# Products of a zero matrix in the open sums of attention 1 and of the convolution of a two-layer graph network

## The chip, the cores and the metric

The kernel runs on one core of one Trainium2 chip. The metric is the time of one launch in microseconds, taken on the device; lower is better. The median of 10 runs of the kernel before is 4104.61 us (lowest 4102.45, highest 4113.44).

## The reference, cut to what matters

A graph has 6250 nodes with 128 features and 200000 edges that are sorted by their destination. Two layers follow each other, both with a residual sum. The first is a graph attention network of two attention layers, the second a convolution over edges:

```
h = relu(layernorm(x))
# attention 1: 4 heads of 16;  attention 2: 1 head of 128
msg = feat[src] * softmax_by_dst(leaky_relu(el[src] + er[dst]))
x = x + segment_sum(msg, dst)                    # (after both attention layers)
h = relu(layernorm(x))
# convolution
w   = einsum(W_tp, gelu(gelu(edge_attr_8 @ W_mlp1) @ W_mlp2))     # weights by edge
mid = concat(m0, m1, m2, m3)       # w * feat[src] * edge_attr_4, 256 numbers by edge
agg = zeros(N, 256).at[dst].add(mid)
x = x + cos * self(h) + sin * (agg @ Wf)
```

The sums over edges by destination (`segment_sum`, `.at[dst].add`) are what the change touches: they are made on TensorE, as products of a 0/1 matrix (edge by node) with the messages, summed in PSUM.

## The kernel before, in words

The edges are cut into tiles of 128, and 8 tiles are a group (`SB = 8`). The rows of the source nodes are fetched by gathers of one tile each, issued by GpSimd (POOL): `gather`, L349 to L353, the issue itself at L351.

**Attention 1** (to about 1590 us of the profile) runs over 117 groups, cut into 8 micro-steps each (`for now in range(NGR * MS + MS)`, L1197). All engines follow the order in which the program is written, recorded under `manual_schedule`; no engine but TensorE's weight loads reorders anything. Three kinds of work are interleaved by micro-step:

- The messages of the group by gathers. `message` (L386) on VectorE (DVE) makes them, ScalarE (ACT) rounds them to a high half (L1226), DVE makes the low half (L1230), `expanded` (L383) gives each edge its node's numbers, `hot` (L356) the 0/1 matrix, and `scatter` (L1154, the product at L1159) adds the group's 8 tiles into the PSUM tile `kept1["acc"]`, 128x136. A chunk of 16 tiles (two groups) is one open sum; when it closes, `evict` copies it by ACT (L1165) and adds it by DVE (L1167). The open sum has one buffer.
- Tables of counts of edges between blocks of nodes: `compare` on DVE (L851), four products a bank on TensorE (L877), eviction by ACT into `ca` (L859), and a DMA to memory (L863). The result of the products has two PSUM buffers, `ca` two in SBUF.
- Dense attention for the other blocks, from the counts: `ramps`, with ACT (L1095), DVE (`clip`, L1019) and TensorE (`add`, L1010 and L1013), and at the end of a pass `close` (L1025, L1027) and `end` (L1040, L1044, L1046). `finish1` (L885 onwards, products L901 and L908) ends four blocks.

In a micro-step the order is: the gathers (m = 0 only), the eviction of a closed sum, the counts' products, the ramps, then `expanded` (m = 3), `hot` (m = 5), `scatter` of one or two tiles of the group before (m = 2 to 7), and the chains of small steps.

**Attention 2** (about 1590 to 2133 us) is dense: TensorE products with bf16 weights at L1414.

**The convolution** (2133 us to the end) runs over 196 groups. For a group, POOL issues 8 gathers (L351), ACT scales the rows (L1494), TensorE makes the hidden layers (`hidden`, L1475) three groups ahead and the weights by edge (`weigh`, L1487) two groups ahead, DVE and ACT make the messages (L1507 to L1541), and `scatter` (L1552) adds the 8 tiles into `state["acc"]`, 128x512 in PSUM. After 24 tiles (`CT`) the sum closes: `close` copies it by ACT (L1582), and `finish3` (L1560 to L1569) transforms it, adds the residual and stores. `sink` tells for each tile whether it starts and whether it closes the sum. Here too the order is that of the program. Per group TensorE has: the first hidden layer of group g + 3, a step of `finish3` if one is due, the second hidden layer, `weigh` of g + 2, and the 8 products of `scatter`. There are six buffers for gathered rows.

```
            first = layers(g + 3)
            next(first, None)
            if not last:
                rows = fetch(g + 1)
            next(first, None)
            pw = big() if hids or todo else None
            if todo:
                todo.popleft().send(pw)
```

Of the kernel before, what the change touches and what calls it, by code (L numbers as in the profile page):

```python
# [32 lines left out]
BF16 = mybir.dt.bfloat16  # L33
# [10 lines left out]
P = 128  # L44
SB = 8
# [3 lines left out]
WSTEP = 16  # L49
HS = 7  # L50
CT, LT = 24, 40
DENSE1 = 20
LAG_D, AFTER, AFTER_D = 14, 12, 5
GP, GK, GSB = 125, 16, 4
# [9 lines left out]
def gnn_kernel(ctx: ExitStack, tc: tile.TileContext, x, src, dst, attr4, attr8,  # L64
# [3 lines left out]
    nc = tc.nc  # L68
# [5 lines left out]
    HD = W1.shape[1]  # L74
    H1, DH = al1.shape
# [17 lines left out]
    NT = src_t.shape[1]  # L93
    NG = NB - DENSE1
    HALF = P // 2
# [16 lines left out]
    keep = tc.keep_in_program_order  # L112

    def big():
        return ps_big.tile([P, 8, P], F32, tag="big", name="big")
# [10 lines left out]
    def whole():  # L126
        return ps_acc.tile([P, 512], F32, tag="acc", name="whole")
# [53 lines left out]
    def load_weights(*pairs):  # L181
        tiles = []
        for name, w in pairs:
            tiles.append(const.tile(list(w.shape), F32, name=name))
            nc.sync.dma_start(tiles[-1], w)
        return tiles
# [488 lines left out]
    keep = lambda ins: ins  # L675
# [40 lines left out]
    def fetch_rows(g):  # L716
        G[g] = gath.tile([P, SB, R1], F32, tag="G", name="G")
        gather(G[g], table1, srcw[:, g * SB:(g + 1) * SB], SB)
# [20 lines left out]
    aw = one.enter_context(tc.tile_pool(name="aw", bufs=2, reuse_waits="tile"))  # L739
# [15 lines left out]
    rhs1 = [dram.tile([P, NB, HW], BF16, name=f"rhs1{q}") for q in range(H1 // 2)]  # L755
    deg1 = pool.tile([P, DENSE1], F32, name="deg1")

# [199 lines left out]
    HH = H1 // 2 * C1  # L957
    assert DENSE1 % 4 == 0
    passes = [(b0, q) for b0 in range(NG, NB, 4) for q in range(H1 // 2)]
# [165 lines left out]
    kept1 = {}  # L1125
# [7 lines left out]
    def chunk_of(g):  # L1133
        return (g * SB + HT // 2) // HT

    def first_of(c):
        return max(0, HT * c - HT // 2)

    def last_of(c):
        return HT * c + HT // 2  # L1140
# [13 lines left out]
    def scatter(g, tiles):  # L1154
        c = chunk_of(g)
        if tiles[0] == 0 and g * SB == first_of(c):
            kept1["acc"] = whole()[:, :2 * (HD + H1)]
        for t in tiles:
            nc.tensor.matmul(kept1["acc"], ohs[g][:, t, :], mss[g][:, t].rearrange("e s f -> e (s f)"),  # L1159
                             start=g * SB + t == first_of(c), stop=g * SB + t + 1 == last_of(c))  # L1160

    def evict(c):
        acc = kept1["acc"]
        ring = fin.tile([P, HD + H1], F32, name="ring", bufs=2)
        nc.scalar.copy(ring, acc[:, :HD + H1])  # L1165
        yield
        nc.vector.tensor_add(ring, ring, acc[:, HD + H1:])  # L1167
        if c:
            b = (c - 1) // 2
            part = slice(0, HALF) if c % 2 else slice(HALF, P)  # L1170
            if c % 2 and b % 4 == 0:
                kept1["sums"] = fin.tile([P, 4, HD + H1], F32, name="sums1", bufs=2)
            nc.vector.tensor_add(kept1["sums"][part, b % 4, :], kept1["ring"][part], ring[part])
            if c % 2 == 0 and (b % 4 == 3 or b == NG - 1):
                chains[0].append(finish1(b // 4 * 4, b % 4 + 1, kept1["sums"][:, :b % 4 + 1, :]))
        kept1["ring"] = ring

    NGR, MS = NT1 // SB, 8
    LEAD = 4
    for c in chunks[:2]:  # L1180
# [16 lines left out]
    for now in range(NGR * MS + MS):  # L1197
        g, m = divmod(now, MS)
        if m == 0 and g + LEAD < NGR:
            fetch_rows(g + LEAD)  # L1200
        if m == 0 and g == 10:
            lin, wm1_sb, wm2_sb, wtp_sb, wf_sb = load_weights(*late_weights)
        done = g >= 2 and (g - 1) * SB == last_of(chunk_of(g - 2))
        if m == 0 and done:
            leaving = evict(chunk_of(g - 2))
            next(leaving)
        due = min(n_banks, n_banks * (now + 1) // ((NGR - AFTER) * MS))
        for _ in range(due - banks):
            next(counting)
        banks = due  # L1210
        if m == 0 and done:
            deque(leaving, 0)
        due = min(n_ramps, max(0, n_ramps * (now + 1 - LAG_D * MS)) // ((NGR - LAG_D - AFTER_D) * MS))
        if due and ramping is None:
            ramping = ramps()
        for _ in range(due - ticks):
            next(ramping)
        ticks = due
        if due == n_ramps:
            next(ramping, None)  # L1220
        if g < NGR:
            if m == 1:
                msg = message(G.pop(g), pes.pop(g))
            if m == 2:
                mss[g] = aw.tile([P, SB, 2, HD + H1], F32R, name="halves")
                nc.scalar.copy(mss[g][:, :, 0, :], msg)  # L1226
            if m == 3 and g + 1 < NGR:
                expanded(g + 1)
            if m == 4:
                nc.vector.tensor_tensor(mss[g][:, :, 1, :], msg, mss[g][:, :, 0, :], op=OP.subtract)  # L1230
            if m == 5 and g + 1 < NGR:
                hot(g + 1)
        if g and m >= 2:
            scatter(g - 1, ((0, 1), (2, 3), (4,), (5,), (6,), (7,))[m - 2])
        for chain in chains:
            advance(chain)
        if evens is None and banks == n_banks:
            assert len(written) == len(steps)
            building.close()
            evens = ahead2.enter_context(tc.tile_pool(name="evens", bufs=1, side="right", reuse_waits="tile"))  # L1240
            pair0 = pair_counts([evens], 0, [nc.sync] * 2), pair_logits([evens], 0)
# [5 lines left out]
    keep = plain  # L1247
    nc.vector.tensor_scalar(wtp_sb[:, 0:3, :], wtp_sb[:, 0:3, :], 1.0 / math.sqrt(HID), None, op0=OP.mult)
    nc.vector.tensor_scalar(wtp_sb[:, 3, :], wtp_sb[:, 3, :], 1.0 / math.sqrt(3.0 * HID), None, op0=OP.mult)
    written_order.close()  # L1250
    nc.vector.tensor_tensor(over1[:, NG:], over1[:, NG:], miscounted(pool, deg1, n_edges[:, NG:], DENSE1), op=OP.max)
    again, some = flags(pool, over1, wide1.to_broadcast([1, NB]))
# [10 lines left out]
    tiles = ctx.enter_context(tc.tile_pool(name="tiles", bufs=1))  # L1263
# [47 lines left out]
    with tc.tile_pool(name="att2", bufs=1) as pool, tc.tile_pool(name="dense", bufs=2) as dense, \  # L1311
# [68 lines left out]
        for b0 in range(0, NB, 2):  # L1380
            n = min(2, NB - b0)
# [10 lines left out]
            acc = big().rearrange("p (k a) c -> p k (a c)", k=2)  # L1392
            if b0 == 8:
                load_tiles(pool)
            for h0 in range(0, NB, HS):
# [7 lines left out]
                c = ct[:, :n, :, h0:h0 + HS, :].rearrange("p k a h d -> p h (k a) d")  # L1403
# [7 lines left out]
                for j, made in ((0, up), (1, down)):  # L1411
                    for h in range(HS):
                        for k in range(n):
                            nc.tensor.matmul(acc[:, k, j * C2:(j + 1) * C2], made[:, h, k * P:(k + 1) * P],  # L1414
                                             rhs2[:, h0 + h, j, :],
                                             start=h0 + h + j == 0, stop=h0 + h + j == NB)
                next(behind, None)
            parts = dense.tile([P, 2, 2, R2], F32, name="parts")
            acc = acc[:, :n, :2 * C2].rearrange("p k (j c) -> p k j c", j=2)
# [30 lines left out]
    cw = ctx.enter_context(tc.tile_pool(name="cw", bufs=2))  # L1450
# [93 lines left out]
    def one_hot3(dl, n, oh):  # L1544
        keep(nc.vector.tensor_tensor(oh[:, :n, :], slot[:, None, :].to_broadcast([P, n, P]),
                          dl[:, :, None].to_broadcast([P, n, P]), op=OP.is_equal))
        return oh

    def scatter(ms, oh, cs, sink):
        for c in cs:  # L1550
            acc, start, stop = sink(c)
            keep(nc.tensor.matmul(acc, oh[:, c, :], ms[:, c].rearrange("e s h i u -> e (s h i u)"), start=start, stop=stop))  # L1552
# [19 lines left out]
    with tc.tile_pool(name="conv", bufs=1) as pool, tc.tile_pool(name="gath3", bufs=6) as gath:  # L1572
# [4 lines left out]
        state, todo = {}, deque()  # L1577
# [12 lines left out]
        def sink(t):  # L1590
            c, k = divmod(t, CT)
            end = min(CT, NT - c * CT) - 1
            if k == 0:
                state["acc"] = whole()
            if k == min(6, end) and c:

                same = cw.tile([P, P], F32, name="same")
                keep(nc.vector.tensor_scalar(same, slot, shift[:, c - 1:c], None, op0=OP.is_equal))
                for a in state["sums"]:
                    keep(nc.tensor.matmul(state["acc"][:, :2 * D], same, a, start=False, stop=False))  # L1600
            return state["acc"], k == 0, k == end

        groups = [(t, min(SB, NT - t)) for t in range(0, NT, SB)]

# [47 lines left out]
        for g, (t, n) in enumerate(groups):  # L1652
            G, g0 = rows
            i = t % LT
            last = g + 1 == len(groups)
            ms, after = messages(G, g0, n, a1s[:, i:i + n, :], pws.popleft(), None if last else lambda: hots(g + 1),
                                 lambda: hids.extend(list(second)[-1:]))
            if i + SB == LT and t + SB < NT:
                a1s = keep_a1(t + SB)
            first = layers(g + 3)  # L1660
            next(first, None)
            if not last:
                rows = fetch(g + 1)
            next(first, None)
            pw = big() if hids or todo else None
            if todo:
                todo.popleft().send(pw)
                next(first, None)
            if t and t % CT == 0:
                close(t // CT - 1)  # L1670
            if hids:
                pws.append(weigh(groups[g + 2][1], hids.popleft(), pw))
            next(first, None)
            scatter(ms, oh, range(n), lambda c: sink(t + c))
            second = first
            oh = after
# [118 lines left out]
```

## Time and profile before

| | |
|---|---|
| median of 10 runs | 4104.61 us |
| the profiled execution | 4109.72 us |
| its span, first to last instruction | 4108.0 us |
| mean granted TensorE clock over the span | 0.812 |
| TensorE busy with products | 2990.8 us (73%) |
| DVE, ACT, POOL busy | 3589.0 (87%), 2791.4 (68%), 2638.6 us (64%) |

The profile is one execution. PE is TensorE's products, PEld its weight loads, SP the queue that issues DMAs. A row of the groups view names the line, the engine, what is written and read, and the number of instructions; then its busy time and the mean time of one, then the idle time of the engine just before them and what ended it. PEclk is the share of TensorE's full clock that was granted. In the records behind it the clock is either 1.0 or 0.5, in stretches that are whole multiples of 3.413 us; such a piece is called a window in what follows.

### The profile page before, as it was taken

To read this page: it belongs to the slowest core of one execution; us is meant where nothing else is said; L and a number is where in the kernel's file an instruction comes from. 1 tells how busy PE (TensorE), PEld (TensorE's weight loads), DVE (VectorE), ACT (ScalarE), POOL (GpSimd) and SP (SyncE) were. 2 spreads that over 40 slices of the span, in tenths; PEclk is the share of its full clock that TensorE was granted. 3 is DMA by queue.
4 is the path that set the end of the run, shared out by engine and by line. 5 is a ranking of instruction groups with operands and counts; after the bars stand their busy time and mean duration, and the time that the engine had idled before them with its cause. 6 is when DMAs were issued, how large, how long until landed. Compare 5 with 4: busy or idle time off the path is not lost. (4 is left out here: it accounts for less than half of the span.)

```text
span 4108.0 us, 61327 instructions
## 1 busy us (share of the span) xinstructions
PE 2990.8 (73%) x19231; PEld 2109.9 (51%) x19232; DVE 3589.0 (87%) x6074; ACT 2791.4 (68%) x6317; POOL 2638.6 (64%) x2568
## 2 busy tenths in 40 slices
PE   4456667676666766999977777777777777777777
PEld 3344445444444446888854444444444444444444
DVE  6888988998888877999969998989998998988997
ACT  3458878887778775999966655555555555555655
POOL 5777877777777770000017777777777777777775
PEclk8557877787777777999988888888888888888888
DMA  4556766776666665444422222222222222222221
GB/s 120 143 168 186 189 168 174 193 186 179 173 166 182 182 180 190 161 166 168 173 79 61 63 62 63 62 62 63 62 63 62 64 62 62 63 62 63 62 62 48
DMA packets 391299, 482.40 MB, mean 117 GB/s; under 512 B 237609, under 2 KB 273300, under 8 KB 390950
## 3 DMA queue, kind: packets, MB, share of 16 engines
q1 hardware_dynamic: 307780, 332.00, 26.7%
q0 software_dynamic: 82400, 144.35, 15.2%
q8 instruction: 159, 2.61, 0.3%
q10 hardware_dynamic: 770, 1.88, 0.2%
q14 instruction: 190, 1.56, 0.1%
HBM read 374.52 MB, written 103.42 MB: 116 GB/s over the span
## 5 line engine op out<-in xcount | busy, mean ns | idle before, releaser
L351 POOL DMA_INDIRECT G<-table,srcc x1563 | 1474.8, 944 | 1018.1 <-DVE kept L1458 542.0
L351 POOL DMA_INDIRECT G<-table,srcw x936 | 1098.7, 1174 | 294.8 <-issue 274.6
L1095 ACT ACTIVATE up<-erb,sel 128x512 bf16<-128x512 f32 x980 | 689.5, 733 | 0.0
L877 PE MATMUL small<-key,lo 128*128 128x98 bf16 x3136 | 339.1, 243 | 254.7 <-ACT ca L859 232.5
L1552 PE MATMUL whole<-halves,ohr 128*128 128x512 f32 x1563 | 501.4, 459 | 0.7 <-ACT acc L1582 0.7
L1494 ACT ACTIVATE g<-G,a 128x128 f32<-128x128 f32 x1563 | 484.4, 393 | 11.1 <-DMA G<-table,srcc 9.1
L859 ACT CAST ca<-small 128x392 bf16<-128x392 f32 x784 | 380.6, 489 | 158.5 <-DMA counts<-ca 100.0
L1010 PE MATMUL up<-up,rc 128*102 128x512 bf16 x980 | 444.9, 475 | 46.1 <-DVE up L1019 20.7
L1401 ACT ACTIVATE ramp<-erb,sel 128x256 bf16<-128x256 f32 (+1 forms) x1138 | 458.2, 493 | 14.4 <-DVE up L1409 9.3
L1487 PEld LDWEIGHTS big<-wtp_sb,hid 64*128 64x128 f32 x3126 | 266.7, 252 | 362.7 <-issue 341.6
L877 PEld LDWEIGHTS <-lo 128*128 128x128 bf16 x3136 | 245.9, 118 | 363.7 <-issue 329.9
L1487 PE MATMUL big<-wtp_sb,hid 64*128 64x128 f32 x3126 | 309.2, 353 | 140.6 <-DVE halves L1541 140.1
L1552 PEld LDWEIGHTS whole<-halves,ohr 128*128 128x128 f32 x1563 | 314.1, 208 | 127.4 <-issue 53.2
L1159 PE MATMUL whole<-halves,ohr 128*128 128x136 f32 x936 | 371.9, 450 | 9.7 <-DVE ring L1167 9.7
L1478 ACT ACTIVATE hid<-layer 128x512 f32<-128x512 f32 x392 | 230.6, 588 | 191.1 <-PE layer L1475 191.1
L1475 PE MATMUL layer<-a8t,wm_sb 16*128 16x512 f32 x392 | 231.6, 672 | 161.8 <-ACT hid L1478 151.8
L1475 PE MATMUL layer<-hid,wm_sb 128*128 128x512 f32 x392 | 337.7, 959 | 14.6 <-ACT hid L1478 12.9
L1532 ACT CAST halves<-mess 128x512 fp32r<-128x512 f32 x195 | 114.3, 586 | 329.8 <-DVE mess L1519 329.8
L1524 DVE TENSOR_TENSOR halves<-mess,halves 128x512 fp32r<-128x512 f32 x391 | 267.8, 685 | 60.2 <-ACT halves L1527 46.9
L1019 DVE TENSOR_TENSOR up<-up,ctc 128x3584 bf16<-128x3584 bf16 x140 | 282.2, 2016 | 28.7 <-ACT up L1095 17.0
L1159 PEld LDWEIGHTS whole<-halves,ohr 128*128 128x128 f32 x936 | 225.5, 259 | 55.2 <-issue 24.9
L1537 ACT CAST halves<-big 128x1024 fp32r<-128x1024 f32 x196 | 197.8, 1009 | 80.5 <-DVE big L1535 80.5
(306 smaller groups left out, 6338.3 us busy)
## 6 DMA issues: line engine op xcount, KB each, us to landing
counts<-ca SPq DMA_DIRECT2D x196, 392.0 KB
ct<-counts SPq DMA_DIRECT2D x196, 392.0 KB
ctc<-counts SPq DMA_DIRECT2D x1120, 56.0 KB
oht<-dlow SPq DMA_DIRECT2D x58, 512.0 KB
rc<-rhs SPq DMA_DIRECT2D x70, 358.8 KB
G<-table,srcc POOLq DMA_INDIRECT x1563
G<-table,srcw POOLq DMA_INDIRECT x936
a8t<-attr_rows SPq DMA_DIRECT2D x391, 16.0 KB
```

The costliest lines, as they stand in the source:

```text
L351: nc.gpsimd.indirect_dma_start(out=G[:, c, :], out_offset=None, in_=table, in_offset=bass.IndirectOffsetOnAxis(ap=idx[:, c:c + 1], axis=0))
L859: nc.scalar.copy(ca[:, :, k * W:(k + WBANK) * W].rearrange("p h (k d) -> p h k d", d=W), ps[:, :WBANK * NKEY].rearrange("p (k h d) -> p h ...
L877: nc.tensor.matmul(ps[:, n * NKEY:(n + 1) * NKEY], lo[:, a, :, r], ky[:, a, :, r], start=True, stop=True)
L1010: nc.tensor.matmul(sums["ups"][j][:2 * C1, :], r[:, i, c:c + 2 * C1], up[:, i], start=h0 + i == 0, stop=h0 + i == NB - 1)
L1019: nc.vector.tensor_tensor(by_part, by_part, state["ct", p, h0].rearrange("p k a h d -> p h (k a) d"), op=OP.min)
L1095: nc.scalar.activation(up[:, i], state["erb", p][:, j], AF.Relu, bias=sel1[:, h0 + i, 2 * q + j:2 * q + j + 1], scale=STEEP)
L1159: nc.tensor.matmul(kept1["acc"], ohs[g][:, t, :], mss[g][:, t].rearrange("e s f -> e (s f)"), start=g * SB + t == first_of(c), stop=g * SB ...
L1401: nc.scalar.activation(ramp[:, h, :n * P], erb[:, :n * P], AF.Relu, bias=sel2[:, h0 + h, :], scale=STEEP)
L1475: keep(nc.tensor.matmul(ph, w, x[:, :npr * P], start=True, stop=True))
L1487: keep(nc.tensor.matmul(pw[:, c, :], hid[half, j * P:(j + 1) * P], wtp_sb[half].rearrange("x p u -> x (p u)"), start=True, stop=True))
L1494: keep(nc.scalar.activation(g0[:, c], G[:, c, :], AF.Copy, scale=a0[:, c, :]))
L1552: keep(nc.tensor.matmul(acc, oh[:, c, :], ms[:, c].rearrange("e s h i u -> e (s h i u)"), start=start, stop=stop))
```

## The change

In attention 1, each micro-step in which a sum is open begins (behind the eviction, ahead of the counts' products) with five products of a 128x128 bf16 matrix of zeros with a column of zeros spread over 136 columns, added into the open sum. In the convolution, each group but the first has ten products of another zero matrix with 512 columns, added into the open sum, between the first hidden layer of group g + 3 and the step of `finish3`, or `weigh` where none is due. The sum that closes is now closed by the last of these ten in the group after, ahead of its copy by ACT; the last tile of all closes by itself.

```diff
+BUSY1 = 5
+BUSY = 10
...
         if tiles[0] == 0 and g * SB == first_of(c):
             kept1["acc"] = whole()[:, :2 * (HD + H1)]
+        kept1["open"] = g * SB + tiles[-1] + 1 < last_of(c)
...
+    nothing1 = aw.tile([P, P], BF16, name="nothing1", bufs=1)
+    nc.vector.memset(nothing1, 0.0)
...
             leaving = evict(chunk_of(g - 2))
             next(leaving)
+        if kept1.get("open"):
+            for _ in range(BUSY1):
+                nc.tensor.matmul(kept1["acc"], nothing1, nothing1[:, 0:1].to_broadcast([P, 2 * (HD + H1)]),
+                                 start=False, stop=False)
         due = min(n_banks, n_banks * (now + 1) // ((NGR - AFTER) * MS))
...
+    nothing = cw.tile([P, P], BF16, name="nothing", bufs=1)
+    nc.vector.memset(nothing, 0.0)
+
+    def busy(acc, n, stop):
+
+        for i in range(n):
+            keep(nc.tensor.matmul(acc, nothing, nothing[:, 0:1].to_broadcast([P, 4 * P]),
+                                  start=False, stop=stop and i == n - 1))
...
-            return state["acc"], k == 0, k == end
+            return state["acc"], k == 0, t + 1 == NT
...
             next(first, None)
+            if t:
+                busy(state["acc"], BUSY, t % CT == 0)
             pw = big() if hids or todo else None
```

In the built program this is 759 x 5 = 3795 products in attention 1 and 195 x 10 = 1950 in the convolution, each with a weight load of its own, and two memsets on DVE. Every other instruction of PE, DVE, ACT, POOL and SP stands in the same order as before. The added products wait for no semaphore.

## The prediction

> **What bounds the kernel now.** I read the page first, then stretches of the span, then the groups and waits of each stretch, and last the timeline around single waits.
>
> ```profile
> PE   4456667676666766999977777777777777777777
> DVE  6888988998888877999969998989998998988997
> POOL 5777877777777770000017777777777777777775
> PEclk8557877787777777999988888888888888888888
> ```
>
> Three stages show: attention 1 (slices 0 to 15), attention 2 (16 to 20, clock full), the convolution. The change adds to TensorE in the first and the last, where its clock is not full. The same by stretches (columns: PE, PEld, DVE, ACT, POOL busy, clock, DMA share, GB/s):
>
> ```profile
> 400.00:1550.00 1150.00, 792.27 (x5650) 556.63 (x5648) 996.90 (x1632) 899.50 (x1763) 878.99 (x732) 0.77 0.67 178
> ...
> 2133.00:4083.00 1950.00, 1483.32 (x6595) 910.66 (x6596) 1749.60 (x2628) 1148.76 (x2726) 1473.91 (x1563) 0.83 0.24 63
> ```
>
> Convolution, POOL's only row there:
>
> ```profile
> L351 POOL DMA_INDIRECT G<-table,srcc x1563 | 1474.8, 944 | 1018.1 <-DVE kept L1458 542.0 <-issue 379.8 <-ACT g L1494 41.7
> ```
>
> The 542.0 us are the wait through attention 2, before the first gather. What is left, 1018.1 - 542.0 = 476.1 us, is 0.305 us ahead of each of 1562 gathers; no gap is over 0.35 us. 1474.8 + 476.1 = 1950.9 us is the whole stretch. **POOL issues gathers without a pause from 2133 to 4083 us, at 8 x 1.249 = 10.0 us a group, and the convolution cannot be shorter than that.** TensorE is not the bound there.
>
> In attention 1 DVE is busy 996.9 of 1150 us and idle 153. POOL waits little (54 us in all), but a group's rows have landed 40 to 60 us before DVE reads them, so it is not the bound. The waits that matter are DVE's and, behind them, ACT's:
>
> ```profile
> DVE ring L1167 <- ACT ring L1165: 51.5, 30, 6.3
> ...
> ACT ca L859 <- PE small L877: 32.4, 40, 1.9
> ...
> ACT ring L1165 <- PE whole L1159: 20.9, 10, 10.8
> ...
> DVE s L1044 <- PE small L1040: 19.8, 12, 3.0
> ...
> DVE lo L851 <- PE small L877: 10.1, 7, 5.4
> ...
> DVE h L912 <- PE small L908: 9.8, 7, 2.5
> ```
>
> DVE waits for TensorE itself in 26 places, 19.8 + 10.1 + 9.8 = 39.7 us. Of the 30 ring waits, 9 (18.8 us) are ones whose ACT copy had itself waited for TensorE. So 35 waits, **58 us, are TensorE's**. I looked up the clock under each: 37.9 of the 39.7 us fall at half clock. One of them in the timeline, with the clock by windows:
>
> ```profile
> 1053.82:1057.24 3.42, 0.35 (x1) 0.06 (x1) 1.96 (x6) 1.86 (x5) 2.58 (x3) 0.50 0.99 310
> 1057.24:1060.65 3.41, 3.41 (x19) 2.46 (x19) 2.16 (x9) 3.41 (x8) 2.64 (x3) 0.50 0.66 237
> ```
>
> ```profile
> 1056.89 0.59 PE L1010 MATMUL up<-up,rc 128*102 128x512 bf16 x1 [5.14 <-ACT some L1027]
> ...
> 1058.46 0.33 DVE L1044 TENSOR_REDUCE s<-small 128x17 f32<-128x51 f32 x2 [2.53 <-PE small L1040]
> ```
>
> TensorE waits 5.14 us for others, loses its clock, and catches up at half speed while DVE waits 2.53 us for it.
>
> **The price of an added product.** No row has a zero operand. The nearest are bf16 products with a weight load each. In attention 2 at full clock, 14 products of L1414 with 196 columns take 1.34 us and one takes 0.248: (1.34 - 0.248) / 13 = 0.084 us each, 0.43 ns a column. So 136 columns take 0.058 us at full clock and 0.113 at half, 512 columns 0.22 and 0.43. A batch in attention 1 is 0.29 or 0.57 us; ten in the convolution 2.2 or 4.3 us. In attention 1 ACT's L1095 takes 726 and 730 ns, DVE's L1019 2016 and 2019 ns with TensorE idle and busy beside it, so I cost no contention. The two memsets, under 0.5 us like DVE's small rows, I leave out.
>
> **Convolution: 0.** TensorE has 1483 / 195 = 7.6 us a group; with 2.2 us it is 9.8 of 10.0, if the clock stays as it is. But the clock falls once a group, after the window in which TensorE waits:
>
> ```profile
> 3006.25:3009.66 3.41, 3.41 (x26) 2.42 (x24) 2.91 (x6) 1.31 (x4) 2.72 (x3) 1.00 0.23 60
> 3009.66:3013.07 3.41, 1.04 (x6) 0.49 (x5) 2.86 (x4) 3.25 (x9) 2.50 (x4) 1.00 0.21 58
> 3013.07:3016.49 3.42, 3.42 (x12) 1.63 (x13) 3.18 (x6) 1.52 (x5) 2.50 (x4) 0.50 0.35 89
> ```
>
> The ten fall into just that window and lift it from 1.04 to about 3.2 of 3.41 us. The 595 us that TensorE is busy at half clock then shrink by about 300, to 6.1 + 2.2 = 8.3 us a group. What the products push back (`finish3`, `weigh`) is needed two groups later. POOL's pace covers all this in both directions: nothing lost, nothing gained. Without that cover (all at half clock) it is 7.6 + 4.3 = 11.9 us a group, 1.9 x 195 = +370 us. The tail after the last gather is on the path: its last sum now closes behind ten products (+2.2 us), and TensorE's 5.7 us of products there at half clock could save 2.8. I take 0, ends -3 and +2.
>
> **Attention 1: -10 us.** From the trace's clock records between 400 and 1550 us: 170 of 337 windows are at half clock. All 82 falls follow a window in which TensorE was busy 0.61 or less (median 0.39); all 82 rises follow one with 0.84 or more. I added to each window the batches that TensorE reaches in it. 38 of the 82 falls then lie above 0.50, and 34 of the 88 half-clock windows that led to another reach 0.85. So 44 falls are left, lasting 1 / (1 - 54/170) = 1.47 windows instead of 2.07: 65 windows instead of 170, about 0.4. The clock would be 0.9 instead of 0.77. The long waits stay: during them TensorE stands at its next instruction, and the zeros queue behind it.
>
> - Six tenths of the 58 us of waits come at full clock and go: -35.
> - There the batches give some back. The TensorE run ahead of such a wait is 3.9 us on average; at half clock a micro-step takes it 448 / 339 = 1.32 us, so a run is 3 micro-steps, 2.4 batches (13 of 16 micro-steps have one): 0.7 of some 1.9 us saved. I take a quarter: +9.
> - Four tenths of the 35 waits, 14, stay at half clock, and grow by 2.4 x 0.57 = 1.4 us: +19.
> - ACT waits 88 us for TensorE, of its 249 idle; the DVE waits that ACT ends by its own lateness (33 ring, 17 up, 8 halves) move with about a third of that: -3.
>
> The sum is -7 - 3 = -10 us. Before 400 us DVE hardly waits for TensorE (3 of 42 us), so nothing there. The ends: all TensorE-ended waits go with ACT's third, -58 - 20 = -78; or none goes and all 35 grow, +49 with ACT's third +65. POOL would allow about -100.
>
> The profiled execution is 4109.7 us, 5.1 above the median. 4109.7 - 10 = 4099.7; against the median 4104.6 the forecast is 4094 us, rounded.
>
> **A rule against this.** The Trainium skill ("TensorE: Matmul & The Clock Gate", Part 1) says that the clock halves after an idle window of about 3.4 us. The trace's falls come at a median of 0.39 busy, so the window agrees and "idle" does not; by the page, topping up half-busy windows would bring 0 and cost the +65. The same part says of a different limiter, of current, that all-zero operands do not trip it; no row here tells whether the clock gate counts zeros.
>
> **The rivals.**
>
> 1. *Clock kept almost everywhere* in attention 1: below 4060, about 4040 (-58 and some of ACT's). For it: 95% of the waits lie at half clock. Against: the long waits hold no batches. 0.12.
> 2. *No change*: the waits for DMA (88.7 us, ACT for the counts' store) and for ACT set attention 1, and gain and loss cancel. 4096 to 4113. 0.27.
> 3. *Slower: the zeros stand ahead of the counts' products in the catch-up runs.* Place: L877 and what follows it in a micro-step. Price 1.4 us for each of 35 waits, with ACT +65: 4115 to 4170. It decides when more than (58 - 15) / (58 - 15 + 49) = 0.47 of the half-clock windows remain; I count 0.4, so it is close. 0.20.
> 4. *The gate does not count zeros*: the change does not do what it is for. Attention 1 as in rival 3, and the convolution at 9.8 of 10.0 us, over it in some groups: 4150 to 4225. 0.07.
>
> **How the numbers follow.** The forecast (4060 to 4096) has 0.34. Faster by over 0.2% (under 4096.4; about what a measurement of this kernel can tell) is 0.34 + 0.12 = 0.46, within 0.2% 0.27, slower 0.27. The range 4055 to 4135 leaves out about 0.1 on each side. The forecast's own range is 4060 to 4096.
>
> **What would show it.** Clock in the convolution 0.93 or more with POOL's row unchanged at 1.249 us a gather; clock in attention 1 near 0.9; DVE's waits for L1040, L877 and L908 down from 39.7 to about 25 us. A clock still at 0.77 and 0.83 is rival 4. A higher clock with more waits for TensorE is rival 3. I am wrong outright if the gathers' pitch changes, or if attention 1's end moves by more than 65 us.

## The result and the profile after

The changed kernel takes **4242.0 us** (median of 8 runs, 4229.3 to 4246.1) against 4105.6 us of the kernel before in the same runs: ratio 1.0326, interval [1.0317, 1.0335]. It is slower, 107 us above the range. The clock rose about as the prediction said; the time did not follow.

The changed kernel's lines have other numbers (L351 is L353, L877 is L879, and so on): the counts' products are L879, `ca` L861, the ring L1168 (ACT) and L1170 (DVE), the zeros of attention 1 L1214; in the convolution the hidden layers are L1484 with ACT's `hid` L1487, the zeros L1564, `finish3`'s first products L1578 with ACT's copy `at` L1580 and its second products L1583, the halves L1533 (DVE) and L1536 (ACT).

The slices of the span after:

```profile
PE   3567777777777777999968888888888888888888
DVE  6888988988888867899968888888888888888887
PEclk7678889888888888999979999999999999999999
```

TensorE is fuller and its clock higher (mean 0.897, before 0.812); DVE shows 8 in every whole slice of the convolution but the last, where it had 9 in more than half. The stretches (columns as in the prediction: PE, PEld, DVE, ACT, POOL busy, clock, DMA share, GB/s), attention 1 and the time from the convolution's first gather to its last:

```profile
400.00:1550.00 1150.00, 858.48 (x8397) 664.59 (x8395) 980.67 (x1590) 893.85 (x1747) 849.54 (x717) 0.87 0.67 177
2168.00:4171.00 2003.00, 1698.57 (x8210) 941.91 (x8337) 1699.08 (x2571) 1121.77 (x2663) 1474.93 (x1563) 0.93 0.24 61
```

The clock rose from 0.77 to 0.87 and from 0.83 to 0.93. But the gathers, 1951 us long before, take 2003 us: their mean pitch went from 1.248 to 1.281 us, with 37 gaps over 0.35 us where there was none. The span's 132.9 us come from three places: attention 1 ends 34.5 us later (the first ramp of attention 2 starts at 1623.8 instead of 1589.3), 1.4 us around attention 2, and 97 us in the convolution (first gather to end 2072.6 instead of 1975.6): 51.6 us in the stretch of the gathers and 45.4 us in the tail behind the last one (70.1 instead of 24.6 us). Before, DVE takes up a group's rows 10 to 17 us after POOL begins to fetch them, all the way. After, this distance grows from 11 us to some 56 us at 3060 us of the span and then stays at 56 to 61; there are six buffers for these rows, and the gaps between the gathers begin there, at 3097 us. So the loss of about the first half shows in the tail, that of the second in the gathers.

**Where the convolution loses.** DVE is idle for 303.9 us of the stretch of the gathers instead of 200.4. Its waits and ACT's there (us in total, times, longest), first before, then after:

```profile
ACT at L1562 <- PE big L1560: 25.6, 36, 1.3
```

```profile
DVE halves L1524 <- ACT halves L1527: 46.9, 84, 1.6
```

```profile
ACT at L1580 <- PE big L1578: 221.8, 62, 4.9
```

```profile
DVE halves L1533 <- ACT halves L1536: 188.0, 57, 4.7
```

One such place in the timeline after (start, duration, engine and line; in brackets the idle time before it and its releaser):

```profile
3018.41 1.12 PE L1484 MATMUL layer<-a8t,wm_sb 16*128 16x512 f32 x2 [3.19 <-ACT hid L1487]
...
3019.46 3.14 PE L1564 MATMUL whole<-nothing 128*128 128x512 bf16 x8
...
3022.55 0.57 DVE L1528 TENSOR_TENSOR mess<-big,g 128x384 f32<-128x384 f32 x1
...
3022.83 0.64 PE L1564 MATMUL whole<-nothing 128*128 128x512 bf16 x1 [0.22 <-issue]
...
3023.25 1.12 PE L1578 MATMUL big<-ident,acc 128*128 128x128 f32 x8
...
3024.41 0.37 ACT L1580 COPY at<-big 128x256 f32<-128x256 f32 x1 [3.25 <-PE big L1578]
...
3025.27 0.60 ACT L1487 ACTIVATE hid<-layer 128x512 f32<-128x512 f32 x1 [0.49 <-PE layer L1484]
3025.77 0.58 ACT L1536 CAST halves<-mess 128x512 fp32r<-128x512 f32 x1
...
3026.38 0.69 DVE L1533 TENSOR_TENSOR halves<-mess,halves 128x512 fp32r<-128x512 f32 x1 [2.72 <-ACT halves L1536]
```

and the clock of the window in which nine of the zeros run, with the window ahead of it (one zero has no record in this trace):

```profile
3016.55:3019.97 3.42, 1.56 (x5) 0.56 (x6) 3.38 (x6) 3.12 (x8) 2.51 (x4) 1.00 0.18 44
3019.97:3023.38 3.41, 3.19 (x9) 1.41 (x9) 3.17 (x6) 1.19 (x4) 2.57 (x3) 0.50 0.28 67
```

TensorE has first waited 3.19 us for ACT's `hid`, is busy for 1.56 of that window's 3.42 us, and its clock falls at 3019.97, just behind the start of the zeros: ten of them take 3.8 us from 3019.46 to the first products of `finish3` at 3023.25. ACT works in the order of the program: its copy `at` waits 3.25 us for these, and the cast L1536 of the running group's messages, whose input was ready at 3023.12 (L1528), stands behind it. DVE waits for the cast. No part of this chain is two groups away. Between copy and cast stands `hid` of the second hidden layer, whose products come behind the same zeros; it waits another 0.49 us, and no run tells the two apart.

**Why that cannot be made up.** A group in which DVE catches up takes it 9.3 us (the lower quartile after is 9.28), POOL needs 10.0 us, so in the three groups of one closed sum DVE can regain at most 3 x 0.7 = 2.1 us, and the cast's wait alone is 188.0 / 57 = 3.3 us. By place in the three, the mean time of a group (from start to start of DVE's L1507, after the change L1516) was 10.03, 9.81 and 10.10 us before and is 9.69, 9.36 and 12.40 after: 31.45 instead of 29.94. That is 1.5 us in each of 65 closed sums, 98 us: the 97 us.

**Attention 1.** The rows of its waits after that answer to those of the prediction:

```profile
DVE ring L1170 <- ACT ring L1168: 52.4, 29, 5.8
ACT ca L861 <- PE small L879: 50.6, 65, 2.7
...
DVE up L1021 <- ACT up L1097: 21.3, 20, 5.0
DVE s L1046 <- PE small L1042: 20.3, 11, 4.0
...
DVE lo L853 <- PE small L879: 14.8, 13, 6.3
...
DVE h L914 <- PE small L910: 11.3, 8, 3.3
```

DVE's direct waits for TensorE are 20.3 + 14.8 + 11.3 = 46.4 us instead of 39.7, although the clock of 0.87 leaves 26% of the time at half clock, 2 x (1 - 0.87), where 0.77 left 46%. By the clock records 33.5 of the 39.7 us ran at half clock before and 30.6 us after, so the part at full clock grew from 6 to 16 us. ACT's `ca` waits 65 times for the counts' products instead of 40.

### The profile page after: what moved, and what is told of

The parts are those of the page before. It is cut to its first block, busy times and chain, and to the rows that moved or that the text cites. A ratio compares the mean times of both kernels' runs of the same rounds, so it can differ in the third digit from the quotient of the medians.

```text
span 4240.9 us, 72692 instructions
## 1 busy us (share of the span) xinstructions
PE 3376.9 (80%) x24847; PEld 2335.6 (55%) x24977; DVE 3580.7 (84%) x6076; ACT 2795.5 (66%) x6317; POOL 2629.9 (62%) x2568
## 3 DMA queue, kind: packets, MB, share of 16 engines
q0 software_dynamic: 82400, 144.35, 14.8%
q14 instruction: 191, 1.56, 0.1%
## 5 line engine op out<-in xcount | busy, mean ns | idle before, releaser
L353 POOL DMA_INDIRECT G<-table,srcc x1563 | 1474.9, 944 | 1071.1 <-DVE kept L1467 543.5
L353 POOL DMA_INDIRECT G<-table,srcw x936 | 1089.4, 1164 | 302.8 <-issue 271.8
L1564 PE MATMUL whole<-nothing 128*128 128x512 bf16 x1821 | 537.2, 443 | 20.6 <-issue 19.0
L861 ACT CAST ca<-small 128x392 bf16<-128x392 f32 x784 | 381.1, 489 | 208.4 <-DMA counts<-ca 108.4
L1570 PE MATMUL whole<-halves,ohr 128*128 128x512 f32 x1563 | 458.3, 428 | 0.7 <-ACT acc L1600 0.7
L1533 DVE TENSOR_TENSOR halves<-mess,halves 128x512 fp32r<-128x512 f32 x391 | 267.7, 685 | 223.7 <-ACT halves L1536 191.1
L879 PE MATMUL small<-key,lo 128*128 128x98 bf16 x3136 | 302.5, 224 | 180.6 <-ACT ca L861 162.0
L1012 PE MATMUL up<-up,rc 128*102 128x512 bf16 x980 | 395.2, 419 | 42.2 <-ACT some L1029 16.4
L1564 PEld LDWEIGHTS <-nothing 128*128 128x128 bf16 x1950 | 197.2, 109 | 412.4 <-issue 277.2
L1484 PE MATMUL layer<-a8t,wm_sb 16*128 16x512 f32 x392 | 235.1, 681 | 224.4 <-ACT hid L1487 214.2
L1214 PE MATMUL whole<-nothing 128*128 128x136 bf16 x3795 | 413.5, 247 | 0.0
L879 PEld LDWEIGHTS <-lo 128*128 128x128 bf16 x3136 | 232.1, 108 | 229.8 <-issue 216.2
L1162 PE MATMUL whole<-halves,ohr 128*128 128x136 f32 x936 | 335.3, 401 | 7.3 <-DVE ring L1170 7.3
L1570 PEld LDWEIGHTS whole<-halves,ohr 128*128 128x128 f32 x1563 | 285.6, 189 | 98.7 <-issue 17.5
L1214 PEld LDWEIGHTS <-nothing 128*128 128x128 bf16 x3795 | 277.4, 110 | 50.6 <-issue 14.6
L1487 ACT ACTIVATE hid<-layer 128x512 f32<-128x512 f32 x392 | 230.6, 588 | 99.1 <-PE layer L1484 99.1
L1496 PEld LDWEIGHTS big<-wtp_sb,hid 64*128 64x128 f32 x3126 | 195.0, 190 | 181.8 <-PE whole L1564 62.4
```

The source lines that it names most:

```text
L353: nc.gpsimd.indirect_dma_start(out=G[:, c, :], out_offset=None, in_=table, in_offset=bass.IndirectOffsetOnAxis(ap=idx[:, c:c + 1], axis=0))
L861: nc.scalar.copy(ca[:, :, k * W:(k + WBANK) * W].rearrange("p h (k d) -> p h k d", d=W), ps[:, :WBANK * NKEY].rearrange("p (k h d) -> p h ...
L879: nc.tensor.matmul(ps[:, n * NKEY:(n + 1) * NKEY], lo[:, a, :, r], ky[:, a, :, r], start=True, stop=True)
L1012: nc.tensor.matmul(sums["ups"][j][:2 * C1, :], r[:, i, c:c + 2 * C1], up[:, i], start=h0 + i == 0, stop=h0 + i == NB - 1)
L1214: nc.tensor.matmul(kept1["acc"], nothing1, nothing1[:, 0:1].to_broadcast([P, 2 * (HD + H1)]), start=False, stop=False)
L1564: keep(nc.tensor.matmul(acc, nothing, nothing[:, 0:1].to_broadcast([P, 4 * P]), start=False, stop=stop and i == n - 1))
```

## The experiments

Two questions. In the convolution: PLACE (the zeros stand ahead of the one product that another engine's queue waits for) against LOAD (TensorE has too much to do). In attention 1: HEAD (the zeros stand ahead of the counts' products, and delay ACT's `ca`) against LOAD (each zero takes TensorE time wherever it stands), and whether the higher clock is worth anything. All kernels start from the changed one, and the diffs are against it. Those whose name begins with a have no zeros in the convolution (the diff of a1b), those with c none in attention 1 (the diff of c1b). The zeros add nothing to a sum, so all of these compute the same. The kernel before took 4104.5, 4105.5 and 4104.4 us in the three sets of runs.

| kernel | zeros | us | ratio, interval |
|---|---|---|---|
| c1b: convolution as changed | 1950 | 4203.3 | 1.0244 [1.0227, 1.0261] |
| c2b: behind `finish3`'s step | 1950 | 4106.3 | 1.0009 [1.0000, 1.0019] |
| c3b: not in the first step's group | 1300 | 4103.9 | 0.9999 [0.9988, 1.0010] |
| c4: not in the second step's group | 1300 | 4244.2 | 1.0341 [1.0324, 1.0358] |
| c5: in the first step's group alone | 650 | 4194.4 | 1.0197 [1.0157, 1.0238] |
| a2: two a micro-step | 1518 | 4117.1 | 1.0025 [1.0015, 1.0036] |
| a1b: five, as changed | 3795 | 4138.9 | 1.0094 [1.0076, 1.0112] |
| a3: five, behind the counts | 3795 | 4150.2 | 1.0108 [1.0091, 1.0125] |
| a10: ten | 7590 | 4201.4 | 1.0233 [1.0216, 1.0251] |
| a4: 24 ahead of `expanded` of a new chunk | 1368 | 4114.9 | 1.0021 [1.0011, 1.0030] |

A first set with the kernels of a1b, c1b, c2b and c3b fell on a chip on which the kernel before itself took 5130 us (4994 to 5232) and the four 5069 to 5335 us; nothing is read from it, and the b marks the repeats.

**The two parts alone.**

```diff
-BUSY1 = 5
+BUSY1 = 0
```

> The convolution's products alone, as in the change. If the two parts add up, the convolution has the whole kernel's loss less attention 1's: 4242 - 34 = 4200 to 4212 us; gathers at a mean pitch of 1.28 us with some 37 gaps over 0.35 us, and over 200 us of ACT's wait for finish3's first products. Well below 4190 would mean that attention 1's products delay the convolution too.

The convolution's part costs 98.8 us, attention 1's (below) 34.4; together 133, the whole change 136.4: they add up to within some 3 us. The gaps and the waits are those of the changed kernel (37 gaps; between 2250 and 4050 us `at` waits 208.9 us for its products, 205.7 us in the changed kernel).

**The same zeros behind `finish3`'s step.**

```diff
-            if t:
-                busy(state["acc"], BUSY, t % CT == 0)
             pw = big() if hids or todo else None
             if todo:
                 todo.popleft().send(pw)
                 next(first, None)
+            if t:
+                busy(state["acc"], BUSY, t % CT == 0)
```

> The convolution's ten zeros alone (none in attention 1), moved behind the step of finish3 and the second hidden layer that follows it, still ahead of the closing copy, of weigh and of scatter. A first run of this kernel fell on a chip on which the kernel before took 5130 us. Theory PLACE (the zeros hold finish3's first product, hence ACT's copy 'at', hence the copy 'halves' queued behind it, hence DVE): the wait of ACT at for PE falls from 227 to about 30 us, DVE is free again, POOL's pitch is 1.249 us and the time 4100 to 4115. Theory LOAD (TensorE has too much work in a group): as with the zeros in their first place, 4190 to 4210.

As many zeros, and the loss is gone: +1.9 us. The same two rows of its waits, in the convolution from 2250 to 4050 us:

```profile
DVE halves L1533 <- ACT halves L1536: 49.0, 61, 1.9
ACT at L1580 <- PE big L1578: 45.0, 49, 1.4
```

No gap between gathers is over 0.35 us and their pitch is 1.248 us. PLACE stands, LOAD falls. The clock is 0.92 there, and still nothing is gained:

```profile
2250.00:4050.00 1800.00, 1626.42 (x7812) 924.32 (x7933) 1624.53 (x2442) 1074.19 (x2531) 1360.54 (x1443) 0.92 0.25 63
```

**Out of one group of the three.** With `CT` 24 and `SB` 8, `finish3`'s first step comes where `t % CT` is 8, its second where it is 16.

```diff
-            if t:
+            if t and t % CT != SB:
```

> The convolution's zeros alone, in the place of the change, but the one group in three whose finish3 step is the first one (t % 24 == 8) has none. PLACE: nearly the whole loss of 97 us goes, 4100 to 4118. LOAD: a third of the zeros less, a third of the loss less, 4165 to 4175.

The loss is gone here too, with the other 1300 zeros in place (`at` waits 63.9 us). The counter-test takes the second step's group out instead:

```diff
-            if t:
+            if t and t % CT != 2 * SB:
```

> The counterpart: the convolution's zeros alone, and the group without them is the one with finish3's second step (t % 24 == 16). As many zeros as in the run before. PLACE: the loss stays, 4185 to 4210. LOAD: 4165 to 4175, as in the run before.

It loses 140 us, more than all 1950 zeros do. The direction is right and the size missed. Its rows (2250 to 4050 us):

```profile
ACT at L1580 <- PE big L1578: 217.9, 56, 4.9
DVE halves L1533 <- ACT halves L1536: 213.5, 88, 4.7
```

The wait of the cast is longer and comes 88 times, the clock is 0.86 instead of 0.93. At 3029.86 us, for one, nine recorded zeros take 3.72 us, half clock again. By place in the three, its groups take 10.09, 9.35 and 12.66 us, those of c1b 9.70, 9.34 and 12.42: 0.64 us in each of 65 closed sums, which is the 41 us of difference. That the lower clock makes it is likely, but not shown by a run of its own.

**In that one group alone.** The sum closes by its last tile again, as in the kernel before.

```diff
-            return state["acc"], k == 0, t + 1 == NT
+            return state["acc"], k == 0, k == end
...
-            if t:
-                busy(state["acc"], BUSY, t % CT == 0)
+            if t % CT == SB:
+                busy(state["acc"], BUSY, False)
```

> Ten products only in the group in which finish3 takes its first step, 65 groups of 196, 650 products. PLACE alone: these are what delays finish3's first products, and without products in the other two groups the clock is lower there, so the loss is at least the change's in the convolution: 4200 to 4260 us. PLACE WITH LOAD: the delay costs only where the next two groups are filled as well and cannot catch up; then POOL's pace takes most of it and the time is under 4150.

A third of the zeros costs 90 us of the 99. Its row of the cast (2133 to 4131 us):

```profile
DVE halves L1533 <- ACT halves L1536: 190.5, 101, 4.7
```

The time is a little under the range expected of PLACE alone and far over 4150; its four runs lie from 4165 to 4203 us, wider than those of the other kernels. So these 650 are enough, and by c3b they are needed.

This run's trace also shows what the place alone costs. In 63 closed sums the zeros stand ahead of `finish3`'s first products between two gathers. In 15 of them all ten run at full clock (2.2 us; the wait for `hid` ahead of them is 0.7 to 2.0 us): the cast is waited for 1.26 us, the group takes 10.5 us and the three groups 29.8 us, within POOL's 30.0. In the other 48 they run at half clock, in part or in whole (3.9 us; the wait for `hid` is 2.1 to 3.8 us): 3.4 us of wait, 12.6 us for the group, 31.9 for the three. The loss is 48 x (31.9 - 30.0) = 91 us, all of it in the sums of the second kind. **So the loss takes the place and the half clock together; at full clock POOL's pace covers the place too.** In c1b and in the changed kernel the ten are at half clock in 62 of these 63 sums. This is a comparison inside one trace; no run was made with the clock alone changed.

**Attention 1 alone, and its dose.**

```diff
-            return state["acc"], k == 0, t + 1 == NT
+            return state["acc"], k == 0, k == end
...
-            if t:
-                busy(state["acc"], BUSY, t % CT == 0)
```

> Zeros in attention 1 alone, none in the convolution. The two stages are separate in the trace (attention 2 begins 34.5 us later, the convolution adds 97 us), so 4105 + 34 = 4139 us, 4130 to 4148.

+34.4 us, as attention 1 in the trace of the whole change (34.5). With the number changed to two and to ten:

```diff
-BUSY1 = 5
+BUSY1 = 2
```

> Two zeros a micro-step in attention 1 instead of five, in the place of the change, none in the convolution. If the loss goes with the zeros' time alone, 34 x 2/5 = +14: 4118 (4112 to 4124). If the clock that the zeros raise gives something back, more than in proportion: 4098 to 4110.

```diff
-BUSY1 = 5
+BUSY1 = 10
```

> Ten zeros a micro-step in attention 1 instead of five, none in the convolution. In proportion to the zeros: 4105 + 68 = 4173 (4160 to 4190). If TensorE becomes the bound (its 0.59 us of zeros in a micro-step of 1.6 on top of 1.1 us), more: over 4190. If the clock, then nearly full, gives back: under 4155.

The loss is 11.6, 34.4 and 95.9 us: 7.6, 9.1 and 12.6 ns for each zero, of the 61 ns or more that it takes TensorE. a2 lies in the range of proportion, a10 above it, in the range given for TensorE as the bound. At none of the three numbers does the clock pay. The stretch of a10:

```profile
400.00:1550.00 1150.00, 944.19 (x10982) 785.26 (x10982) 963.52 (x1563) 885.32 (x1720) 827.62 (x699) 0.93 0.65 173
```

At clock 0.93 the stage is the slowest of the four: DVE's idle time in attention 1 (from 100 us on) is 210.6 us before, 228.7 with two, 235.3 with five and 292.8 with ten zeros. What grows with the number is work behind TensorE: from none to ten, ACT's `ca` waits 46.5, 61.3, 79.4 and 112.7 us for the counts' products, and its ring copy 22.6, 27.8, 31.3 and 41.9 us for the scatter's. Of the 82 us that DVE is idle for longer with ten, waits for ACT make up 60 and direct waits for TensorE 27, while waits for DMA fall by 7. The instructions of the other engines are not slower for it: ACT's ramps (L1095) take 733 ns before and 729 with ten, DVE's `clip` (L1019) 2016 and 2017.

**Behind the counts' products.** The five move three lines down in the micro-step.

```diff
-        if kept1.get("open"):
-            for _ in range(BUSY1):
...
         for _ in range(due - banks):
             next(counting)
         banks = due
+        if kept1.get("open"):
+            for _ in range(BUSY1):
...
```

> Zeros in attention 1 alone, the five of a micro-step moved from ahead of the counts' four products to behind them (still ahead of the ramps' products and of scatter). In the run with the zeros ahead of them (4139 us), ACT's wait of ca for PE small had grown from 46.5 to 78 us. Theory HEAD (the zeros ahead of the counts' products delay them, hence ACT's eviction, hence DVE): 4104 to 4115. Theory LOAD (TensorE's work by micro-step is what counts, the next micro-step's counts stand behind these zeros anyway): 4130 to 4145.

+44.7 us: HEAD falls, and the time is 5 us above the range of LOAD. Its two rows of ACT:

```profile
ACT ca L861 <- PE small L879: 37.8, 46, 2.1
...
ACT ring L1168 <- PE whole L1162: 24.4, 17, 9.6
```

The wait of `ca` does shrink (50.6 in the changed kernel), and the loss goes elsewhere: over the whole stage ACT's ring copy waits 40.4 us instead of 31.3, DVE's ring 65.4 instead of 55.1. In both places something next in TensorE's queue is late by the zeros.

**In the wait itself.** TensorE's long waits are for `oht`, ahead of `expanded` of a chunk's first group; the clock falls in them. Here no micro-step has zeros, and 24 stand just ahead of that product instead.

```diff
-BUSY1 = 5
+BUSY1 = 24
...
-        if kept1.get("open"):
-            for _ in range(BUSY1):
...
             if m == 3 and g + 1 < NGR:
+                if (g + 1) * SB == first_of(chunk_of(g + 1)) and kept1.get("open"):
+                    for _ in range(BUSY1):
+                        nc.tensor.matmul(kept1["acc"], nothing1, nothing1[:, 0:1].to_broadcast([P, 2 * (HD + H1)]),
+                                         start=False, stop=False)
                 expanded(g + 1)
```

> Zeros in attention 1 alone, and none by micro-step: 24 of them (1.4 us at full clock) in one place of every second group, directly ahead of the products of a new chunk's expanded, where TensorE waits 2.2 us on average for DVE's oht (37 waits, 81 us between 400 and 1550 us). If a clock kept through a wait is worth something, and zeros cost nothing there: 4085 to 4100, clock in attention 1 over 0.80. If the clock is worth nothing to DVE: 4102 to 4108. If the zeros overrun the wait: 4112 and more.

The clock behind the wait is kept: at the start of `expanded` it is half in 3 of 45 places between 400 and 1550 us, before in 26, and it is 0.84 over the stage. But it costs 9.4 us. The 24 zeros overrun the wait: `expanded` starts 1.06 us after `oht` is ready on average, before 0.39. That this makes the whole loss is not shown: in the two traces attention 1 ends only 2.2 us later. And DVE's direct waits for TensorE are 49.1 us, 34.4 of them at half clock (33.5 before), so the falls that this avoids are not those under DVE's waits.

## Why the prediction was wrong

- **The price of a zero product: right.** From the traces the pitch is 0.061 and 0.113 us with 136 columns and 0.218 and 0.427 us with 512, at full and half clock; the estimates were 0.058, 0.113, 0.22 and 0.43.
- **The gate counts zeros: right; the clock: right in the convolution, a little too high in attention 1.** 0.93 in the convolution (0.93 said), 0.87 in attention 1 (0.9 said). Rival 4, that they do not count, is out. But the prediction's 170 half-clock windows were misread: the clock of 0.77 in the row it shows, and the records, give 157 of 337. After the change 84 are left, 0.54 of them and not 0.4. That is above the 0.47 at which the prediction itself turns to slower: its own sum with 0.54 gives about +6, or +8 with ACT's third, and not -10.
- **Convolution, 0: this is the step that failed worst,** at "What the products push back (`finish3`, `weigh`) is needed two groups later. POOL's pace covers all this in both directions." It is true of what `finish3` stores and of the weights. It is not true of ACT's copy `at` of `finish3`'s first products: that sits in ACT's queue ahead of the running group's casts, and DVE reads those at once. I followed the data, not the queue. The result is +97 instead of 0, and c2b, c3b and c5 show that one place makes it, by c5's trace with the zeros at half clock there. The cover had a second end that I did not work out: DVE needs 9.3 of POOL's 10.0 us, so 0.7 us a group is all that can be lost and regained.
- **The sum by the clock in the convolution was half right, and the other half is the term that broke the cover.** "The ten fall into just that window and lift it" holds for two groups in three: there the ten run at full clock. In the first step's groups the wait for `hid` lies just ahead of the ten, the clock falls as they start, and they run at half clock themselves (3.8 us, where the sum had 2.2). At the 2.2 us of the sum the cover would have held, by the 15 sums of c5.
- **Convolution's bound as a bound: right.** Where nothing is pushed into that chain (c2b, c3b), POOL's pitch stays at 1.248 us and the time does not move, with 1300 to 1950 zeros more.
- **Attention 1, -10: the failed term is "six tenths of the 58 us of waits come at full clock and go: -35".** The clock rose about as said (0.87, said 0.9), but I took the falls that vanish to be spread over the waits. They are not: of DVE's direct waits for TensorE, 33.5 us ran at half clock before and 30.6 after. Nor do the waits go that come at full clock: these went from 6 to 16 us, and with ten zeros, at a clock of 0.93, they are 37 us, with 20 at half clock. So "and go" failed as well as the six tenths. A likely reason for the first is that such a wait sits in a run that follows a long wait of TensorE, in which it stands at an instruction and has no zeros to run, as the prediction said of itself ("the long waits hold no batches") without drawing the consequence.
- **The give-back (+9, +19) was too small, and ACT's share (-3) had the wrong sign.** The dose runs price it: 7.6 to 12.6 ns a zero, +34 for 3795, more through ACT's `ca`, ring and casts than through DVE's direct waits. The upper end +65 held the +34.5.
- **Rival 3 had the right sign and stage, and its place was wrong:** the counts' products are not what decides, by a3. What the dose and a3 point to is TensorE's time as such, in a stage where its order is fixed and the other engines wait for whatever is next. Its condition, more than 0.47 of the half-clock windows left, was met.

The table of the experiments also answers rival 2: no change is what the zeros give in the convolution once they are out of one chain. Rival 1, a clock kept almost everywhere, comes nearest in a10, and there the time is 4201 us. No kernel here beats the one before; the best, c3b, is at 0.9999 [0.9988, 1.0010].

What stays open: why the groups of c4 are slower than those of c1b with more zeros, which single chain carries the loss in attention 1, and whether a full clock exactly under DVE's waits for TensorE (33.5 us at half clock) would pay. The last needs products that run while TensorE waits and stop when the wait ends; a fixed number ahead of the wait (a4) overran it.

## What to carry to other kernels

Before an instruction that is pushed back is costed at nothing, look in the queue of the engine that reads its result for what stands behind that reader: here the queue that keeps the program's order made everything behind it wait, however late the result itself was needed. Cost an added instruction at the clock of its own place: behind a wait of 3.2 us the ten took 3.8 us and not 2.2, and in c5's trace only the sums where they did so lost time. A cover by another engine's pace is worth only the gap to the next slowest engine, here 0.7 us a group. Filler that keeps TensorE's clock up can pay only if the clock is raised under the very waits that cost time; look up which windows these are, and which of them the filler can reach, before counting a share of all. Even then the filler stands in the same queue: with ten zeros most of DVE's direct waits came at full clock, and they were longer in all.

## What the hardware showed that was not expected

Products of an all-zero matrix raise the granted clock (0.77 to 0.93 with ten in a micro-step). A clock of 0.93 instead of 0.77 over a whole stage, or of 0.92 instead of 0.84 in the convolution (c2b), gave no time back in this kernel. The Trainium skill ("TensorE: Matmul & The Clock Gate", "Why this matters for your kernels") advises for throughput to keep TensorE busy and to leave it no idle gaps above about 3 us; the traces agree that more products hold the clock (82 falls in attention 1 before, 55 after), and the times show that it is no aim in itself.
